# An attention and expert block on one core: the last rows kept on chip, first gathers split around the last tile, tables by large VectorE operations

## The chip, the core and the metric

One core of a Trainium2 chip runs the whole block as one program. Its engines have queues of their own: TensorE (PE, with the weight load shown apart as PEld), VectorE (DVE), ScalarE (ACT), GpSimd (POOL) and SyncE (SP), which only issues DMAs. The metric is the device time of one execution in microseconds, the median of several runs. All times below are microseconds unless they are marked ns.

## The reference, cut to what matters

The input is 32 samples of 256 tokens of 256 channels. A first part (a gate from a condition, causal attention over the 256 tokens of a sample, a low-rank conditioned layer) ends in rows `x` of 256 channels. The second part runs attention across the 32 samples at each token position, and then a layer of eight experts with a limit on the rows that each may take:

```python
attn = jax.nn.softmax(scores, axis=-1)
...
proj = jnp.einsum('sbh,oh->sbo', ao, proj_weight)
h1 = hidden_states + proj
ln2 = _layer_norm(h1, ln2_weight, ln2_bias)
...
probs = jax.nn.softmax(x @ router_weight, axis=-1)
top_p, top_i = jax.lax.top_k(probs, K)                 # K = 2 of E = 8
...
dst = jnp.where(within < cap, sorted_exp * cap + within, T)
...
fc1 = jax.nn.gelu(jnp.einsum('ech,ehf->ecf', xt, moe_w1))
fc2 = jnp.einsum('ecf,efh->ech', fc1, moe_w2).reshape(T, H)
...
return h1 + moe_out.reshape(S, B, H)
```

There are 8192 rows; each goes to its two best experts, 16384 rows of work, less those over the limit.

## The kernel before

**Stage 1** (loop at L476) handles one sample per step. It ends in a tile `o` of 128 partitions with the rows of the sample, two tokens to a partition, and POOL writes it to a DRAM array `xx_d[token, sample, :]` (L464). Three buffers `rows` hold `o` in turn.

**Stage 2** (loop at L1184, i from -13 to 64) works on 64 tiles of 128 rows, each 4 tokens x 32 samples. The order is written out by hand: at step i each helper is called for the tile for which it is due. Rows come back from `xx_d` in groups of four tiles, 16 groups in all; the first three (`EARLY`) have tiles of their own that exist already in stage 1, and their samples 0 to 27 are fetched ahead (`fetch_steps`, L107). When stage 2 begins, SP fetches samples 28 to 31 of these three groups, four DMAs a group at L111. A tile is then normalised on ACT (L762), turned and projected on PE, scored, masked on DVE (L820, L827) and POOL (L828), turned again (`turn_scores`, L837, and L842), multiplied with the values (L849) and put out (L883). Per group, `normalise2` and `judge` compute the second norm and the router's logits, and `rows2` and `store` write rows to DRAM for the experts.

**Placing the rows.** `route` picks the two best experts; it writes a 0/1 array `hot` for first and second choice. The place of each row within its expert's blocks is a running count. So that experts may start early, tiles 0 to 47 of the first ten samples (`SURE`) of each position are placed first: `packed(q)` compacts their choices onto 120 partitions with four small DMAs (L995), and `early()` counts them and makes the **first table**, the row numbers for the first eleven blocks of 256 rows (`EARLYB`). `rest()` does the same for all that is left, the **second table**. A table is made by matmuls: for eight row positions at a time, DVE makes a one-hot `oh` of the place within a block (L1125, L1438) and eight one-hots `wid` of the block multiplied with the row number, one operation each (L1132, L1446); a matmul for each position adds `oh` x `wid` into PSUM (L1140, L1431). The first table has 4 such groups, the second 16. Two integer operations (`rows_of`, L1164) then turn the sum into the row numbers `src_row` that a gather needs.

`early`, `rest`, `route` and `packed` are Python generators in a list `todo`. `advance(us)` emits their instructions into the stream until the costs that they yield come to its budget; a bare `yield None` ends that portion, so that the next matmul stands later than its input. At i = 61 whatever is left of the first table is emitted at once, and then the gathers of blocks 0 to 2 (POOL, L658, two indirect DMAs each) and the weights of block 0.

**Stage 3** (L1499, n from 0 to 19, `AHEAD`) computes one block of 256 rows a turn: `hidden(n)` (16 matmuls at L690 and two Gelus at L694), a gather for block n+3, `turn_in(n+1)` (L676 on PE, L680 on DVE), `weights(n+1)` (the expert's number is loaded into a register of DVE, and DVE copies 128 x 2048 floats at L668), `advance(HALF)`, `result(n)` (16 matmuls at L702, a copy on ACT at L706, a store by SP), and `advance(HALF)` again. At n = 10 (`EARLYB - 1`) the rest of the second table is emitted at once and the gathers of blocks 11 to 13 follow. Further blocks and the combining of each row's two results (`yg`, L1553) come behind.

Of the kernel before, what the change touches and what calls it, by code (L numbers as in the profile page):

```python
# [10 lines left out]
I32 = mybir.dt.int32  # L11
# [27 lines left out]
HALF = 2.4  # L39
# [10 lines left out]
def block_kernel(ctx: ExitStack, tc: tile.TileContext, a: dict, out: bass.AP):  # L50
# [56 lines left out]
    def fetch_steps(sg, lo, hi):  # L107

        src = xx_d[16 * sg : 16 * sg + 16].rearrange("(j b) s e -> b s j e", j=4)
        for b in range(4):  # L110
            nc.sync.dma_start(  # L111
                out=live2[sg]["xx"][32 * b + lo : 32 * b + hi], in_=src[b, lo:hi]
            )


    with ExitStack() as c1:
# [359 lines left out]
        for s in range(S + 1):  # L476
# [12 lines left out]
            if s == 5:  # L489
# [26 lines left out]
                with tc.tile_pool(name="cst", bufs=1) as cst:  # L516
# [14 lines left out]
                    for b in range(4):  # L531
# [12 lines left out]
                    icolf = cst.tile([P, P, 8], F32, name="icolf")  # L544
                    nc.gpsimd.iota(
                        icolf, pattern=[[1, P], [0, 8]], base=0, channel_multiplier=0,
# [12 lines left out]
                    icol = bf("icol_b", icolf)  # L559
                    irow = bf("irow_b", irowf)  # L560
                freshc = const.tile([P, NE, PACK], BF16, name="freshc")
# [4 lines left out]
                nc.vector.tensor_scalar(rowbits, rowbits, 16, None, ALU.logical_shift_left)  # L566

                rowbitsc = const.tile([P, PACK], I32, name="rowbitsc")
                for q in range(3):
                    for b in range(4):  # L570
                        r = SURE * (4 * q + b)
                        nc.sync.dma_start(
                            out=rowbitsc[r : r + SURE],
                            in_=rowbits[32 * b : 32 * b + SURE, PACK * q : PACK * (q + 1)],
                        )
# [41 lines left out]
            if s > 0:  # L617
                low_rank(s - 1)
            if s < S:
                transpose_p(s)  # L620
# [11 lines left out]
    hot = keep.tile([P, NJ, 2, NE], BF16, name="hot")  # L632
# [8 lines left out]
    hotc = keep.tile([P, PACK, 2, NE], BF16, name="hotc")  # L641
    slots1 = keep.tile([P, NJ, 2], F32, name="slots1")
    in1 = keep.tile([P, NE, 3 * PACK], BF16, name="in1")
    nc.gpsimd.memset(slots1, 0.0)
    nc.gpsimd.memset(in1, 0.0)

# [6 lines left out]
    ereg = nc.vector.alloc_register("ereg")  # L653
# [10 lines left out]
    def weights(n):  # L664
        eid, at_ = (eids[0], n) if n < EARLYB else (eids[1], n - EARLYB)
        nc.vector.load(ereg, eid[0:1, at_ : at_ + 1], bass_reorder=False)
        e = nc.vector.snap(ereg, min_val=0, max_val=NE - 1)
        nc.vector.tensor_copy(  # L668
            wcs[n % 2].rearrange("p a f -> p (a f)"),
            wall[:, bass.ds(e, 1), :, :].rearrange("p e a f -> p (e a f)"),  # L670
        )
# [58 lines left out]
    with ExitStack() as c2:  # L730
# [15 lines left out]
        def fetch(sg):  # L746
            if sg < EARLY:
                return fetch_steps(sg, 28, S)
# [186 lines left out]
        def route(first, n):  # L935
# [12 lines left out]
            revb = rev.unsqueeze(1).to_broadcast(je)  # L948
            left, val = lg, []
            cost = 0.22 if n > 8 else 0.19  # L950
            for k in range(2):
# [11 lines left out]
                nc.vector.tensor_tensor(hot[:, js, k, :], revb, over_e(rk), ALU.is_equal)  # L963
                yield cost
                if k == 0:
                    left = tmp("r_left", [NE])
                    nc.vector.scalar_tensor_tensor(
                        left, hot[:, js, 0, :], NEG, lg, ALU.mult, ALU.add
# [4 lines left out]
                both[:, :, js].rearrange("p e j -> p j e"), hot[:, js, 0, :], hot[:, js, 1, :],  # L973
                ALU.add,
# [14 lines left out]

        def packed(q):  # L990

            yield from route(PACK * q, PACK)
            for b in range(4):
                r = SURE * (4 * q + b)
                nc.sync.dma_start(  # L995
                    out=hotc[r : r + SURE],
                    in_=hot[32 * b : 32 * b + SURE, PACK * q : PACK * (q + 1)],
                )

        def early():  # L1000
# [11 lines left out]
            def by_expert(t):  # L1012
                return t[:, : NE * PACK].rearrange("p (e j) -> p e j", e=NE)

            ej = [NR, NE, PACK]

            def over_j(t):
                return t[:NR].unsqueeze(2).to_broadcast(ej)

            bothc, prec = cut(2 + NE * PACK, BF16), cut(NE * PACK, BF16)  # L1020
            nc.vector.memset(bothc[:, 0:1], 0.0)
            chosen = bothc[:, 1 : 1 + NE * PACK]
            nc.vector.tensor_tensor(
                by_expert(chosen)[:NR].rearrange("p e j -> p j e"), hotc[:NR, :, 0, :],
                hotc[:NR, :, 1, :], ALU.add,
            )
            yield 0.3
            nc.vector.tensor_tensor_scan(
                prec[:NR], bothc[:NR, : NE * PACK],
# [13 lines left out]
            for t in (prec, chosen):  # L1043
# [5 lines left out]
            yield None  # L1049
# [25 lines left out]
            ofk = yss[0].rearrange("p a b -> p (a b)")[:NR, : PACK * 2 * NE].rearrange(  # L1075
                "p (j k e) -> p j k e", k=2, e=NE
            )
            nc.vector.tensor_tensor(
                ofk, hotc[:NR],
                by_expert(slot)[:NR].rearrange("p e j -> p j e").unsqueeze(2)  # L1080
                .to_broadcast([NR, PACK, 2, NE]), ALU.mult,
            )
            yield 0.5
            n2 = 2 * PACK
            slots = cut(n2)
            nc.vector.tensor_reduce(
                slots[:NR].rearrange("p (j k) -> p j k", k=2), ofk, AX.X, ALU.add
            )
            none, col = cut(n2), cut(n2)
# [30 lines left out]
            for g in range(n2 // 8):  # L1120
# [10 lines left out]
                for i in range(8 * g, 8 * g + 8):  # L1131
                    nc.vector.tensor_scalar(  # L1132
                        wid[:NR, nbc * i : nbc * (i + 1)], irow[:NR, :nbc], col[:NR, i : i + 1],
                        rowbitsc[:NR, i // 2 : i // 2 + 1].bitcast(F32), ALU.is_equal, ALU.mult,
                    )
                    yield 0.1
# [11 lines left out]

        def split(pi, ci, hi, part, col, where):
# [9 lines left out]
            nc.vector.tensor_tensor(col, ci, hi, ALU.add)  # L1159
# [9 lines left out]
        def experts_of(late, cnt, cnti, diag, i=0, ps=None):  # L1169
# [10 lines left out]
            yield None  # L1180
# [3 lines left out]
        for i in range(-13, NJ + 1):  # L1184
# [8 lines left out]
            advance(0.2 if i < 3 * PACK + 2 else 1.2)  # L1193
            if 0 <= i + 3 < NJ:
                project(i + 3)
            if 0 <= i < NJ:
                values(i)
            if i == NJ:
# [11 lines left out]
            at(i, 5, normalise2)  # L1210
            at(i, 6, judge)
            for j in range(4):
                at(i, j + 6, rows2, j)
# [11 lines left out]
            if i == NJ - 3:  # L1225
# [9 lines left out]
                for n in range(3):  # L1235
                    gather(n)
                weights(0)
# [7 lines left out]
    with tc.tile_pool(name="rt", bufs=1) as rt, tc.tile_pool(  # L1245
# [8 lines left out]
        def by_tile(t):  # L1254

            return t.rearrange("p g e -> p e g").unsqueeze(3).to_broadcast([P, NE, NSG, 4])

# [9 lines left out]
        def rest():  # L1267
# [16 lines left out]
            yield None  # L1284
            kept = keptp[:, 1:].rearrange("p (e j) -> p e j", e=NE)
            nc.vector.scalar_tensor_tensor(
                keptp[:, 1:], p_row.rearrange("p e j -> p (e j)"), float(CAP), bothp[:, 1:],
                ALU.is_lt, ALU.mult,
            )
            yield 0.7  # L1290

            head = kept[:, :, : 3 * PACK]
            nc.vector.tensor_tensor(head, head, in1, ALU.subtract)
            yield 0.4
# [19 lines left out]
            yield None  # L1314
# [28 lines left out]
            last = [t1(f"last{i}", NSG + 1) for i in range(2)]  # L1343
            for t in last:
                nc.vector.memset(t[:, 0, :], 0.0)
            nc.vector.tensor_tensor(last[0][:, 1:, :], off, some, ALU.mult)
            yield 0.4
            step, at_ = 1, 0
            while step < NSG:
                src, dst = last[at_], last[1 - at_]  # L1350
                nc.vector.tensor_copy(dst[:, 1 : 1 + step, :], src[:, 1 : 1 + step, :])
                nc.vector.tensor_tensor(
                    dst[:, 1 + step :, :], src[:, 1 + step :, :],
                    src[:, 1 : NSG + 1 - step, :], ALU.max,
                )
                yield 0.4
                step, at_ = 2 * step, 1 - at_
            last = last[at_]
            jump = t1("jump")
            nc.vector.tensor_tensor(jump, last[:, 1:, :], last[:, :-1, :], ALU.subtract)  # L1360
# [4 lines left out]
            yield 0.5  # L1365
# [7 lines left out]
            nc.vector.tensor_tensor(slot4, slot4, by_tile(jump), ALU.mult)  # L1373
            yield 0.65
            nc.vector.tensor_tensor(slot4, slot4, by_tile(last[:, :-1, :]), ALU.add)
# [11 lines left out]
            jke = [P, NJ, 2, NE]  # L1387
            of_k = rt.tile(jke, F32, name="of_k")
            nc.vector.tensor_tensor(
                of_k, hot, slot.rearrange("p e j -> p j e").unsqueeze(2).to_broadcast(jke),  # L1390
                ALU.mult,
            )
            yield 1.9
            n2 = 2 * NJ
            slots = rt.tile([P, n2], F32, name="slots")
            nc.vector.tensor_reduce(
                slots.rearrange("p (j k) -> p j k", k=2), of_k, AX.X, ALU.add
            )
            yield 1.2
# [8 lines left out]
            col = rt.tile([P, n2], F32, name="col")  # L1408
            ints = [rt.tile([P, n2], I32, name=f"int{i}") for i in range(3)]
            split(*ints, part, col, where)  # L1410
            yield 1.2
# [14 lines left out]
            p_tab = rps.tile([P, nbc], F32, name="p_tab", tag="long")  # L1426
            ready = []
            for g in range(n2 // 8 + 1):
                for oh, wid, k in ready:
                    for i in range(8):  # L1430
                        nc.tensor.matmul(  # L1431
                            p_tab, lhsT=oh[:, :, i], rhs=wid[:, i, :],
                            start=(k == 0 and i == 0), stop=(k == n2 // 8 - 1 and i == 7),
                        )
                ready = []
                if g < n2 // 8:
# [3 lines left out]
                        part[:, 8 * g : 8 * g + 8].unsqueeze(1).to_broadcast([P, P, 8]),  # L1440
# [3 lines left out]
                    for i in range(8):  # L1444
                        j = 4 * g + i // 2
# [220 lines left out]
```

## Time and profile before

| | us |
|---|---|
| median of 3 runs | 1193.61 (1191.83 to 1194.23) |
| the profiled execution | 1260.33 |
| its span | 1258.6 |
| PE busy in it | 1118.8 (89%) |
| POOL busy | 539.4 (43%) |
| DVE busy | 702.3 (56%) |
| ACT busy | 399.5 (32%) |
| mean granted TensorE clock | 0.925 |

The profiled execution is one run, and it is 66.7 us longer than the median; what is read from it is compared with itself. Busy shares are averages over stages with different limits, so the stages are read one by one. These are the largest groups of instructions beside the ones for the tables; the columns are line, engine, operation, output and input with their shapes, count, then busy time and mean ns of one, then idle time of the engine just before and what ended most of it:

```profile
L702 PE MATMUL ps_y<-xx,ht 128*128 128x256 f32 x864 | 218.6, 410 | 48.1 <-ACT ht L694 41.1
L690 PE MATMUL ps_h<-xt,xx 128*128 128x256 f32 x864 | 197.9, 382 | 6.1 <-DVE xx L668 4.5
L658 POOL DMA_INDIRECT xx<-z_d,src_row x108 | 119.5, 1106 | 148.8 <-issue 83.1
L1553 POOL DMA_INDIRECT yg<-y_d,yrow x128 | 135.8, 1061 | 128.7 <-DMA y_d<-ys 67.8
```

A line names a tile by the buffer that it lies in: gathered rows and the expert weights use the memory of `xx`, and the first table's `oh` and `wid` that of `ht` and `xt`.

### The profile page before, as it was taken

To read this page: it belongs to the slowest core of one execution; us is meant where nothing else is said; L and a number is where in the kernel's file an instruction comes from. 1 tells how busy PE (TensorE), PEld (TensorE's weight loads), DVE (VectorE), ACT (ScalarE), POOL (GpSimd) and SP (SyncE) were. 2 spreads that over 40 slices of the span, in tenths; PEclk is the share of its full clock that TensorE was granted. 3 is DMA by queue.
4 is the path that set the end of the run, shared out by engine and by line. 5 is a ranking of instruction groups with operands and counts; after the bars stand their busy time and mean duration, and the time that the engine had idled before them with its cause. 6 is when DMAs were issued, how large, how long until landed. Compare 5 with 4: busy or idle time off the path is not lost. (4 is left out here: it accounts for less than half of the span.)

```text
span 1258.6 us, 17522 instructions
## 1 busy us (share of the span) xinstructions
PE 1118.8 (89%) x5926; PEld 913.4 (73%) x5926; DVE 702.3 (56%) x1781; ACT 399.5 (32%) x958; POOL 539.4 (43%) x798
## 2 busy tenths in 40 slices
PE   5999999999994999999988699989987996688692
PEld 4988888888872777777766488768876875566581
DVE  5135555555552888888899868842223543233342
ACT  2023333333333566666654122112211221111120
POOL 4012222222222566666665452043254775754562
PEclk8589999999997999999999699979997997988896
DMA  9023333333253143443341141022233663553554
GB/s 327 10 64 103 120 113 109 102 108 120 73 144 115 36 149 123 170 166 116 129 159 46 60 138 55 27 69 73 76 106 113 204 189 103 155 152 114 152 167 128
DMA packets 84867, 147.45 MB, mean 117 GB/s; under 512 B 11272, under 2 KB 51360, under 8 KB 84256
## 3 DMA queue, kind: packets, MB, share of 16 engines
q1 hardware_dynamic: 68832, 97.92, 23.9%
q0 software_dynamic: 15936, 48.32, 12.7%
q8 instruction: 49, 0.80, 0.3%
q14 instruction: 50, 0.41, 0.1%
HBM read 89.39 MB, written 56.69 MB: 116 GB/s over the span
## 5 line engine op out<-in xcount | busy, mean ns | idle before, releaser
L702 PE MATMUL ps_y<-xx,ht 128*128 128x256 f32 x864 | 218.6, 410 | 48.1 <-ACT ht L694 41.1
L702 PEld LDWEIGHTS ps_y<-xx,ht 128*128 128x128 f32 x864 | 174.0, 207 | 78.8 <-ACT ht L694 45.7
L680 DVE TENSOR_SCALAR xt<-ps_xt,ln 128x256 f32<-128x256 f32 x106 | 52.8, 541 | 273.7 <-PE ps_xt L676 139.9
L690 PE MATMUL ps_h<-xt,xx 128*128 128x256 f32 x864 | 197.9, 382 | 6.1 <-DVE xx L668 4.5
L1553 POOL DMA_INDIRECT yg<-y_d,yrow x128 | 135.8, 1061 | 128.7 <-DMA y_d<-ys 67.8
L690 PEld LDWEIGHTS ps_h<-xt,xx 128*128 128x128 f32 x864 | 164.6, 191 | 31.1 <-DVE xx L668 5.6
L658 POOL DMA_INDIRECT xx<-z_d,src_row x108 | 119.5, 1106 | 148.8 <-issue 83.1
L706 ACT COPY ys<-ps_y 128x512 f32<-128x512 f32 x54 | 31.7, 587 | 272.9 <-PE ps_y L702 125.7
L694 ACT ACTIVATE ht<-ps_h 128x512 f32<-128x512 f32 x108 | 63.8, 598 | 145.4 <-PE ps_h L690 85.8
L94 POOL TENSOR_SCALAR ve<-mv 128x2 f32<-128x2 f32 (+2 forms) x49 | 10.8, 220 | 221.0 <-DVE mv L102 219.8
L778 PE MATMUL p_qkv<-wqkv,lnt 128*128 128x384 f32 x256 | 94.5, 493 | 0.0
L828 POOL TENSOR_TENSOR sc<-sc,mx 128x512 f32<-128x512 f32 x64 | 67.7, 1058 | 53.1 <-DVE mx L827 46.0
L849 PEld LDWEIGHTS p_av<-vbd,pt 128*128 128x128 f32 x512 | 68.0, 196 | 27.4 <-ACT pt L842 13.1
L788 ACT COPY vbd<-p_qkv 32x64 f32<-32x64 f32 x256 | 52.9, 207 | 91.1 <-DVE qk L784 88.8
L849 PE MATMUL p_av<-vbd,pt 128*128 128x68 f32 x512 | 67.0, 275 | 8.1 <-ACT pt L842 5.9
L883 PE MATMUL p_pr<-wp,ao 128*128 128x264 f32 x256 | 72.7, 407 | 0.0
L340 PE MATMUL p_z<-yt,m_qk 128*128 128x256 f32 x256 | 69.3, 396 | 1.3 <-ACT yt L329 1.3
L668 DVE COPY xx<-wall 128x2048 f32 x54 | 66.8, 1236 | 1.4 <-DMA xx<-z_d,src_row 1.4
L888 POOL TENSOR_TENSOR res<-h,xx 128x256 f32<-128x256 f32 x64 | 43.8, 685 | 51.8 <-DVE h L887 51.6
L453 PE MATMUL p<-layer,x1t 128*128 128x264 f32 x256 | 64.0, 393 | 0.8 <-ACT x1t L443 0.7
L369 DVE TENSOR_TENSOR layer<-p_l,base 128x264 f32<-128x264 f32 x64 | 24.7, 428 | 69.7 <-PE p_l L364 69.7
L349 PE MATMUL p_v<-w_vo,yt 128*128 128x256 f32 x256 | 61.2, 382 | 0.0
(301 smaller groups left out, 1981.3 us busy)
## 6 DMA issues: line engine op xcount, KB each, us to landing
xx_d<-o POOLq DMA_DIRECT2D x32, 530.0 KB
y_d<-ys SPq DMA_DIRECT2D x54, 256.0 KB
xx<-xx_d SPq DMA_DIRECT2D x13, 1060.0 KB
xt<-in_x_t_dram SPq DMA_DIRECT2D x32, 256.0 KB
xs<-in_x_dram SPq DMA_DIRECT2D x32, 256.0 KB
wall<-in_moe_w_dram SPq DMA_DIRECT2D x16, 512.0 KB
z_d<-h SPq DMA_DIRECT2D x16, 512.0 KB
res_d<-res SPq DMA_DIRECT2D x16, 512.0 KB
```

The source lines that it names most:

```text
L340: nc.tensor.matmul(p_z[:, m, :], lhsT=m_qk[:, c, m * P : (m + 1) * P], rhs=yt[:, c, :], start=(c == 0), stop=(c == 1),)
L453: nc.tensor.matmul(p_2, lhsT=v["x1t"][:, c, t * P : (t + 1) * P], rhs=v["layer"][:, c, :], start=(c == 0), stop=(c == 1),)
L658: nc.gpsimd.indirect_dma_start(out=xgs[n % 4][:, h, :], out_offset=None, in_=z2_d[: 3 * PACK * P, :] if n < EARLYB else z2_d[:, :], in_off ...
L668: nc.vector.tensor_copy(wcs[n % 2].rearrange("p a f -> p (a f)"), wall[:, bass.ds(e, 1), :, :].rearrange("p e a f -> p (e a f)"),)
L690: nc.tensor.matmul(ps[:, i, :], lhsT=we1[:, c, f * P : (f + 1) * P], rhs=xts[n % 2][:, c, :], start=(c == 0), stop=(c == 1),)
L694: nc.scalar.activation(hts[n % 2][:, 2 * f2 : 2 * f2 + 2, :], ps, AF.Gelu_apprx_tanh)
L702: nc.tensor.matmul(ps[:, h, :], lhsT=hts[n % 2][:, f, h * P : (h + 1) * P], rhs=we2[:, f, :], start=(f == 0), stop=(f == 3),)
L778: nc.tensor.matmul(ps, lhsT=live2[n // 4]["lnt"][:, c, j * P : (j + 1) * P], rhs=wqkv[:, c, :], start=(c == 0), stop=(c == 1),)
L828: nc.gpsimd.tensor_tensor(sc, sc, mx.unsqueeze(2).to_broadcast([P, 16, S]), ALU.subtract)
L849: nc.tensor.matmul(p_a[:, g // 2, :, g % 2, :], lhsT=v["pt"][:, g, :], rhs=vbd[n % 5][:, g], start=True, stop=True,)
L883: nc.tensor.matmul(p_p, lhsT=tiles[n]["ao"][:, gp, :], rhs=wp2[:, gp, :], start=(gp == 0), stop=(gp == 1),)
L1553: nc.gpsimd.indirect_dma_start(out=yg, out_offset=None, in_=y_d[:upto, :], in_offset=bass.IndirectOffsetOnAxis(ap=yrow[:, j, k : k + 1], a ...
```

## The change

**The last rows.** At the end of stage 1, samples 28 to 30 of the first three groups are fetched from DRAM, those of the first group on the ACT queue and the others on SP. Sample 31 isn't read back: twelve small DMAs copy it from its tile on chip to the three groups. `fetch` in stage 2 leaves these groups out.

**The tables.** `hot` becomes `hot1`, which holds only the first choice; the second is had by subtraction. `packed` moves two arrays instead of one (eight DMAs). The eight `wid` operations of a group become two, `columns` (a comparison) and `numbered` (a multiplication with the row numbers, now in bf16); in the first table all four groups share one pair of them. In the second table the groups are made in pairs with the matmuls of a pair one portion later. A chain of four copies and maxima becomes one scan, and some bare yields are gone.

**The order.** `advance` comes behind `project` and `values`, with 1.4 instead of 1.2, and `HALF` is 3.2 instead of 2.4. At i = 61 only block 0 is gathered. The gathers of blocks 1 and 2, the weights of block 0 and a new subtraction on POOL (`other`) stand at i = 63, and two helpers of the last groups are moved by a step or two.

**The weights.** For the first eleven blocks the register is loaded and the weights are copied by ACT, for the later ones by DVE as before.

```diff
-HALF = 2.4
+HALF = 3.2
...
+            if s == S:
+                for sg in range(EARLY):
+                    fetch_steps(sg, 28, S - 1, nc.sync if sg else nc.scalar)
+
+                for sg in range(EARLY):
+                    for b in range(4):
+                        (nc.sync if sg or b % 2 else nc.scalar).dma_start(
+                            out=live2[sg]["xx"][32 * b + S - 1 : 32 * (b + 1)],
+                            in_=rows[(S - 1) % 3][16 * sg + b : 16 * (sg + 1) : 4, 0, :],
+                        )
...
-        nc.vector.load(ereg, eid[0:1, at_ : at_ + 1], bass_reorder=False)
-        e = nc.vector.snap(ereg, min_val=0, max_val=NE - 1)
-        nc.vector.tensor_copy(
+        i = int(n >= EARLYB)
+        eng, copy = ((nc.scalar, nc.scalar.copy), (nc.vector, nc.vector.tensor_copy))[i]
+        eng.load(eregs[i], eid[0:1, at_ : at_ + 1], bass_reorder=False)
+        e = eng.snap(eregs[i], min_val=0, max_val=NE - 1)
+        copy(
...
-                nc.sync.dma_start(
-                    out=hotc[r : r + SURE],
-                    in_=hot[32 * b : 32 * b + SURE, PACK * q : PACK * (q + 1)],
-                )
+                for t, u in ((both, by_expert(bothc[:, 2:])), (hot1, hot1c)):
+                    nc.sync.dma_start(
+                        out=u[r : r + SURE],
+                        in_=t[32 * b : 32 * b + SURE, :, PACK * q : PACK * (q + 1)],
+                    )
...
+        def columns(out, col, n):
+
+            k = col.shape[1] // 2
+            dims = [col.shape[0], k, n // 2, 2]
+            nc.vector.tensor_tensor(
+                out.rearrange("p (k n h) -> p k n h", k=k, h=2),
+                irow[: dims[0], :n].rearrange("p (n h) -> p n h", h=2).unsqueeze(1)
+                .to_broadcast(dims),
+                col.rearrange("p (k h) -> p k h", h=2).unsqueeze(2).to_broadcast(dims),
+                ALU.is_equal,
+            )
+
+        def numbered(rows, bits):
+
+            k = bits.shape[1]
+            rows = rows.rearrange("p (k n h) -> p k n h", k=k, h=2)
+            nc.vector.tensor_tensor(
+                rows, rows, bits.unsqueeze(2).to_broadcast(rows.shape), ALU.mult
+            )
...
-            advance(0.2 if i < 3 * PACK + 2 else 1.2)
             if 0 <= i + 3 < NJ:
                 project(i + 3)
             if 0 <= i < NJ:
                 values(i)
+            advance(0.2 if i < 3 * PACK + 2 else 1.4)
...
-                for n in range(3):
+                gather(0)
+            if i == NJ - 1:
+                weights(0)
+                for n in range(1, 3):
                     gather(n)
-                weights(0)
+                nc.gpsimd.tensor_tensor(other, both[:, :, : 3 * PACK], in1, ALU.subtract)
...
-            for g in range(n2 // 8 + 1):
-                for oh, wid, k in ready:
...
+            for g in range(0, n2 // 8 + 2, 2):
+                for r in ready:
+                    passes(*r)
                 ready = []
-                if g < n2 // 8:
+                for k in range(g, min(g + 2, n2 // 8)):
...
-                    for i in range(8):
-                        j = 4 * g + i // 2
-                        nc.vector.tensor_scalar(
-                            wid[:, i, :], irow[:, :nbc], col[:, 8 * g + i : 8 * g + i + 1],
-                            rowbits[:, j : j + 1].bitcast(F32), ALU.is_equal, ALU.mult,
-                        )
-                    yield 1.5
-                    ready.append((oh, wid, g))
-                    if g % 2 or g == n2 // 8 - 1:
-                        yield None
+                    rows = wid.rearrange("p i n -> p (i n)")
+                    columns(rows, col[:, 16 * k : 16 * k + 16], nbc)
+                    numbered(rows, rb2[:, 4 * k : 4 * k + 4])
+                    ready.append((oh, wid, k))
+                    yield 1.8
+                yield None
```

## The prediction, made before the changed kernel was run

> **What bounds the kernel now.** I read the engine totals first: TensorE is busy for 1118.8 of 1258.6 us, so the time is its work plus its pauses, and only a pause can be won. The row of slices shows where they are. Each digit is the share in tenths of 31.5 us, so a digit under 9 is a pause:
>
> ```profile
> PE   5999999999994999999988699989987996688692
> ```
>
> The 4 at slice 12 is the change of stage. The dips at slices 20 to 22 are the end of stage 2 and the first table of rows, the 8 at 25 is the second table, and the late ones lie among the experts, which the change hardly touches. The view of windows prices them. Its columns are window, length, busy time of PE, of the weight load, of VectorE, ScalarE and GpSimd, then granted TensorE clock and DMA:
>
> ```profile
> 384.00:395.00 11.00, 0.00 (x0) 0.00 (x0) 0.00 (x0) 0.02 (x1) 2.08 (x7) 0.50 0.26 72
> 420.00:640.00 220.00, 220.00 (x1460) 168.57 (x1458) 191.59 (x464) 136.74 (x359) 142.62 (x242) 1.00 0.41 142
> 636.80:690.80 54.00, 46.95 (x304) 34.05 (x302) 49.97 (x132) 24.85 (x70) 29.28 (x51) 1.00 0.23 77
> 690.80:728.30 37.50, 24.73 (x118) 19.30 (x117) 27.96 (x97) 6.99 (x13) 17.01 (x25) 0.68 0.16 50
> 728.30:802.50 74.20, 72.87 (x388) 63.27 (x387) 58.05 (x161) 17.62 (x31) 22.41 (x22) 1.00 0.26 89
> 802.50:830.80 28.30, 20.29 (x113) 15.40 (x112) 24.00 (x90) 2.53 (x5) 3.79 (x4) 0.76 0.08 24
> ```
>
> The 220 us of full tiles have no pause: a tile takes 4.52 us and VectorE has some 0.7 us of it to spare. From 636.8 to 728.3 VectorE is the limit (49.97 of 54.0), and at 802.5 again. So the change works in three places, at 384, 637 to 728 and 802. I price each against the profiled execution (1260.33 us, 1.7 more than its span). That run lies 67 us above the median of 1193.61, mostly in long pauses after 920 us; the three places lie ahead of them, so I carry the gain over whole.
>
> **Part 1, the change of stage.** The timeline (start, duration, instruction, idle time before it and its releaser):
>
> ```profile
> 385.16 0.81 POOL L464 DMA_DIRECT2D xx_d<-o  x1 [0.30 <-POOL o L463]
> 388.55 6.50 SPq L111 DMA_DIRECT2D xx<-xx_d  x12
> 394.98 1.59 ACT L762 ACTIVATE z<-xx 128x256 f32<-128x256 f32 x3 [15.22 <-DMA xx<-xx_d]
> ```
>
> Stage 2 waits for the last sample's rows to go to DRAM (385.16 to 388.55) and return through twelve fetches, 0.54 us to issue each; the first group's fourth is issued at 390.2, and its data is used at 394.98, 4.8 us on. After the change rows 28 to 30 need only sample 30's write, landed near 381.7. Sample 31's rows go straight from the tile on the chip, complete at 384.86. ScalarE, idle until 394.98, issues four of the first group's and two of its last copies (385 to 386); SP issues the other eight fetches (381.7 to 386), then two copies to 387.1. Landing takes 3.1 us (write end to the first semaphore) to 4.5 us, so the data is there near 391: **4 us** gained. Here a rule speaks against the change: the Trainium skill, "DMA: Bandwidth & Descriptors", section "Issuing engines are not separate DMA queues", says that issuing from several engines shares the same DMA engines and saves only issue time, usually small beside the transfer. By the rule the second queue is worth about nothing, and the removed DRAM trip (3.4 us) alone pays. The row has 6.5 us of issue against some 4 of landing, so it isn't small; I take 4 instead of 3. The bounds are 0 (a stage 2 buffer waits for memory that the late copies still read; 24 are issued until about 391) and 6.
>
> **Part 2, the end of stage 2.** In the chain here, `L837` turns the scores of a tile, `L1132` is the first table and `L668` the weights:
>
> ```profile
> 698.92 1.66 DVE L1132 TENSOR_SCALAR xt<-irow_b,z,rowbitsc 120x22 bf16<-120x22 bf16 x8
> 705.07 1.08 PE L837 MATMUL ps_t<-ident,sc 128*128 128x128 f32 x4
> 710.17 1.23 DVE L668 COPY xx<-wall 128x2048 f32 x1 [1.35 <-DMA xx<-z_d,src_row]
> 715.16 1.11 PE L837 MATMUL ps_t<-ident,sc 128*128 128x128 f32 x4 [4.42 <-POOL sc L828]
> ```
>
> Before: tile 61 starts at 690.8, tile 62 14.3 us later because the table is drained at i=61, tile 63 10.1 after that (its mask sits behind the weight copy on VectorE and six gathers on GpSimd), and the first result 13.1 later, at 728.3. After: counting the generator's steps with its new costs, the table is complete at i=60, so the drain finds nothing. I take 5.2, 4.4 and 13.4 us, the last 0.3 longer because two gathers and the 0.8 us subtraction now stand ahead of the residual on GpSimd. That wins 14.5.
>
> But the work comes into tiles 51 to 60. They took 54.0 where PE alone needs 45.2; the 8.8 over it plus ten slacks of 0.7 is 15.8 us of added VectorE time. Now come four comparisons (4 x 0.68 = 2.7), the two large operations for 704 elements (about 0.52 each, 1.05) and some of the router's next pass (1.6); the dropped `chosen` and the longer slot sums cancel. Add 1.5 for waiting on the 32 table matmuls, 0.7 for a two-input operation held while GpSimd works (1.10 us for a 128-element one at L1070), and a **new wait**: the scan at i=53 needs eight compacting DMAs, not four. The four of L995 take 3.02 us to issue, so eight take 6, and the last lands some 8 us after the tile's start, but VectorE is at the scan after 3.8, so about 3.7 is lost; queued behind the scan are the next mask and the query copies. Sum 27.0, less 7 of slack: 20.0 over 45.2, against 8.8. It gives back 11.2, so **3.3 us** stay. The bounds are +9 (no scan wait, slack used better) and -4 (both the DMA wait and contention doubled).
>
> **Part 3, the second table.**
>
> ```profile
> L1438 DVE TENSOR_TENSOR oh<-icol_b,part 128x1024 bf16<-128x1024 bf16 x16 | 11.1, 692 | 0.0
> L1446 DVE TENSOR_SCALAR wid<-irow_b,col,rowbits 128x126 bf16<-128x126 bf16 x128 | 30.2, 321 | 0.0
> 826.04 0.95 POOL L658 DMA_INDIRECT xx<-z_d,src_row  x1 [57.14 <-issue]
> 830.81 5.42 PE L702 MATMUL ps_y<-xx,ht 128*128 128x256 f32 x16
> ```
>
> A group is one `oh` and eight `wid`, spaced at 2.39 us. Six of sixteen are drained at n=10 while PE runs dry, and the next result starts 28.3 us after the transpose at 802.5. The rule against it: "VectorE: DVE Perf Modes" of the Trainium skill, section "The perf-mode tier table (the rule you actually need)", has a two-tensor operation stop at two elements a cycle where a one-tensor operation reaches four. By the rule, and since there are now two passes over 1008 elements, the swap costs more. But 321 ns for 126 elements is mostly fixed cost, and eight take 1.9. The nearest row for the new operations is `oh`, of the same kind and size, 0.692: by length 0.68 each, so the group is 2.05 busy, about 1.9 spaced. At one element a cycle it would be 1.2 each, group 3.0. I take 0.68: the pairs keep the innermost run contiguous as in `oh`. The first groups then come at n=3 instead of 5, fourteen are done by n=9, two remain. From the transpose of n=10: passes to 5.6, hidden to 9.1, passes to 12.0, row numbers 12.9, gather 13.5, result 4.8 later at 18.3; **10.0 us** less. Three more groups' passes come before 802.5 (1.44 for two, so 2.2), a wait on the expert count of 0.5 and less cold clock go the other way: 8.6 net. The bounds are 4 and 11. What is late next is the gather, 4.8 us that nothing shortens.
>
> **The weights on ScalarE.** `ys` takes 587 ns for 512 elements and `vbd` 207 for 64: 0.85 an element, so 1.9 us for 2048 against 1.24 on VectorE. They stand behind both Gelus of a block and are done about 2.9 us after them; the hidden layer needs them 4.2 after. Result copies queue behind, with over 3 us to spare. ScalarE is busy for 17.6 of 74.2. Cost nothing; without that cover 0.65 x 11 = 7.
>
> **The rest**, smaller index tables and setup under full stage 1 work, fewer small operations: nothing. Sum 4 + 3.3 + 8.6 = 15.9: 1260.3 to about 1244.4, and the median to **1178**.
>
> **Rivals.**
> *More* (0.17): the scan does not wait and the boundary gives 6: 6 + 7 + 9.5 = 22.5, 1171. For: VectorE's order before the scan isn't tight. Against: eight small DMAs in one queue.
> *Mostly given back* (0.17): late buffers at the boundary (1), early table -1, one element a cycle (5): 1188.5. For: tiles 51 to 60 already run on VectorE.
> *Slower* (0.05): the weight copy on ScalarE becomes the limit of a block. It decides beyond about 4.3 us from the second Gelu; at 6 us eleven blocks lose 1.7 each, 19, so 15.9 turns into -3: 1197. Against: it would need three times the rate of its rows.
> *Not doing what it says* (0.06): the pauses after 920, 10 to 20 us each and not explained by a release, fall differently and cover the gain: 1188 to 1200.
>
> My forecast has 0.55, its own range 1172 to 1184. The range of 1167 to 1191 reaches over both near rivals. A measurement of this kernel can tell about 0.2% from no change; the cases give 0.87 faster, 0.05 within, 0.08 slower.
>
> **What would show it.** First `z` near 391; the scan at i=53 idle for some 3 to 4 us on a compacting DMA; no matmul of the first table between tiles 61 and 62, and tile 62 about 5 us after 61; second table groups spaced at 1.9 with 0.68 a large operation, two of them left at n=10, result 18 after the transpose; the ScalarE weight copy near 1.9 and no wait of the hidden layer on it. The prediction is wrong if the tiles 51 to 60 take over 75 us, or the large operations over 1 us.

## The result and the profile after

The changed kernel takes 1177.15 us (median of 4 runs, 1176.11 to 1181.11) against 1193.92 before: ratio 0.9866, 95% interval 0.9837 to 0.9894, 16.8 us less. The forecast was 1178. The profiled execution has a span of 1174.4 us. The total was right, in part by luck: by the positions below, part 1 gave 3.4 us less than forecast and parts 2 and 3 gave 2.7 and 4.3 more, while the time moved 2.7 less than the parts add up to.

The row of slices of the changed kernel (a slice is 29.4 us) and its windows, with the same columns as before: tiles 51 to 60; tiles 61 and 62; tile 63 to the first result; blocks 0 to 8; block 9 to 10:

```profile
PE   5999999999999599999999788998999999999891
```

```profile
637.06:697.07 60.01, 48.65 (x336) 36.60 (x334) 52.87 (x145) 25.26 (x70) 29.59 (x51) 1.00 0.21 69
697.07:707.48 10.41, 6.06 (x42) 4.50 (x40) 9.37 (x28) 1.68 (x3) 5.63 (x7) 1.00 0.37 133
707.48:722.52 15.04, 11.57 (x44) 9.14 (x45) 6.32 (x24) 6.71 (x10) 10.55 (x18) 0.77 0.12 37
722.52:796.50 73.98, 72.92 (x415) 63.91 (x414) 50.34 (x110) 34.23 (x41) 17.59 (x23) 1.00 0.27 90
796.50:812.70 16.20, 11.10 (x87) 9.86 (x86) 11.23 (x29) 4.14 (x6) 3.78 (x4) 0.97 0.13 42
```

The tiles at 637 are slower than before (54.0), still on VectorE; tiles 61 and 62, which had 24.4 us with a clock near 0.65, now take 10.4 at full clock; block 9 to 10 fell from 27.9 to 16.2. Set beside the two profiles, in us:

| step | forecast | measured |
|---|---|---|
| last write of stage 1 to the first tile's turned scores | 4 less | 21.94 to 21.38: 0.6 less |
| tiles 51 to 60 | 11.2 more | 53.99 to 60.01: 6.0 more |
| tile 61 to 63 | 14.8 less | 24.37 to 10.41: 14.0 less |
| tile 63 to the first result | 0.3 more | 13.14 to 15.04: 1.9 more |
| first result to that of block 9 | 1.4 more | 74.62 to 73.98: 0.6 less |
| block 9 to 10 | 10.0 less | 27.89 to 16.20: 11.7 less |
| block 10 to 11 | 0 | 9.14 to 8.56: 0.6 less |
| sum | 15.9 less | 19.5 less |

Three things the numbers need. Stage 1 itself ended 0.8 later in this execution, so block 11 starts 18.7 earlier. Two rows of the table also move between executions of the kernel before: in its second profile (`b_again`, below) tiles 51 to 60 take 56.75 and tile 63 to the first result 15.34, so that the gain from the last write to block 11 is 17 to 25 us, by the pair of profiles that is taken. And executions differ by some 80 us from one occasion to another, the kernel before included (1276 and 1272 us in the first two sets of runs below, 1194 in the third), nearly all of it behind block 11. So ratios are given against the kernel before of the same set, and the readings rest on positions ahead of block 11.

### The profile page after: what moved, and what is told of

The parts are those of the page before. It is cut to its first block, busy times and chain, and to the rows that moved or that the text cites. A ratio compares the mean times of both kernels' runs of the same rounds, so it can differ in the third digit from the quotient of the medians.

```text
span 1174.4 us, 17424 instructions
## 1 busy us (share of the span) xinstructions
PE 1083.7 (92%) x5926; PEld 894.6 (76%) x5926; DVE 674.0 (57%) x1641; ACT 419.8 (36%) x969; POOL 539.1 (46%) x800
## 4 chain that ended last, share of the span: by engine, by line
PE 73%; issue 9%; DMA 7%; DVE 6%; POOL 3%; SPq 1%; ACT 1%; POOLq 0%; DVEq 0%; ACTq 0%
PE ps_h L713 10%; PE ps_y L725 9%; PE p_qkv L801 6%; PE p_z L340 5%; PE p L453 5%; PE p_v L349 5%; PE p_pr L906 4%; PE p_av L872 4%; DMA yg<-y_d,yrow 4%; PE p_sc L831 3%; PE ps_t L860 3%; PE p_o L422 3%; DMA xx<-z_d,src_row 3%; PE p_s L389 2%; POOL yg L1608 2%
## 5 line engine op out<-in xcount | busy, mean ns | idle before, releaser
L725 PE MATMUL ps_y<-xx,ht 128*128 128x256 f32 x864 | 200.2, 386 | 0.0
L679 POOL DMA_INDIRECT xx<-z_d,src_row x108 | 124.1, 1149 | 134.5 <-issue 66.5
L725 PEld LDWEIGHTS ps_y<-xx,ht 128*128 128x128 f32 x864 | 163.6, 194 | 21.1 <-ACT ht L717 0.3
L801 PEld LDWEIGHTS p_qkv<-wqkv,lnt 128*128 128x128 f32 x256 | 44.7, 195 | 18.6 <-issue 1.2
```

The lines of the kernel that those rows point to most:

```text
L679: nc.gpsimd.indirect_dma_start(out=xgs[n % 4][:, h, :], out_offset=None, in_=z2_d[: 3 * PACK * P, :] if n < EARLYB else z2_d[:, :], in_off ...
L725: nc.tensor.matmul(ps[:, h, :], lhsT=hts[n % 2][:, f, h * P : (h + 1) * P], rhs=we2[:, f, :], start=(f == 0), stop=(f == 3),)
L801: nc.tensor.matmul(ps, lhsT=live2[n // 4]["lnt"][:, c, j * P : (j + 1) * P], rhs=wqkv[:, c, :], start=(c == 0), stop=(c == 1),)
```

## The experiments

### Which part of the time is the kernel's

`b_again` is the kernel before once more; `after_again` and `after_third` are the changed kernel, each for the runs beside it.

> The kernel before, unchanged, for a second profile: that of the prediction was 67 us above its median. Theory (the 67 us are pauses of that one execution after 920 us, and the change wins only ahead of block 11): span near 1192, the start of block 11's result near 840 as in the first profile, and from there to the end some 352 us, as the changed kernel has (821.3 to 1174.4, 353). Rival (the change also shortens the tail, by its later loads of the weights or less traffic): from block 11 to the end 360 us or more.

It took 1283 us. Its block 11 starts at 849.3, 9 us later than in the first profile (stage 1's last write is 4 late, tiles 53 and 54 are 3 longer, and tile 63 to the first result 2 longer), and 432 us lie behind it, against 419 in the first profile. My theory of one bad execution fell. So did the rival, though its sign came: the changed kernel has 432 there too (`after_again`), so the long tail goes with the occasion.

> The changed kernel once more, on one chip with the next three, so that they can be set beside it. Theory (its gain lies ahead of block 11, whatever the chip): ratio to the kernel before 0.984 to 0.988; last write of stage 1 to first z 8.8 us, tile 53's period 8.3, first result to that of block 9 74.0, block 9 to 10 16.2. Rival (the step from block 3 to 4, 8.7 in the first profile and 11.7 in two of the experiments, differs from run to run of one kernel): that step is 11.7 here too.

> The changed kernel, for the run above. Theory: ratio to the kernel before 0.984 to 0.988, and the positions of its stages within 1.5 us of its two earlier profiles.

The ratios were 0.9848 (0.9784 to 0.9913) and 0.9846 (0.9822 to 0.9870). The positions held within the bounds, but for block 1 to 2 of `after_again`, 9.25 in place of 8.05, where VectorE waited 2.9 for a signal of PE. From block 11 to the end it was 432 and 355. Where the 432 go can be seen in a pause, here from the timeline of `e2_group_by_group` (described below), at a result copy of ScalarE:

```profile
1021.22 0.59 ACT L727 COPY ys<-ps_y 128x512 f32<-128x512 f32 x1 [15.09 <-remote]
```

The copy waits for two marks, that of the store that last read its buffer, two blocks back, and TensorE's. TensorE's came at 1021.15, 12 us after the recorded end of the matmuls that it stands for (1009.0). The last landing that the trace has of that store is at 995.56, and its record is incomplete. What made the signal late isn't shown.

### The change of stage

The timeline of the changed kernel, and what SP's queue waited for (total, times, longest):

```profile
382.57 8.64 SPq L111 DMA_DIRECT2D xx<-xx_d  x8
382.60 1.51 ACTq L111 DMA_DIRECT2D xx<-xx_d  x4
385.94 0.81 POOL L464 DMA_DIRECT2D xx_d<-o  x1 [0.30 <-POOL o L463]
386.37 2.40 ACTq L633 DMA_DIRECT2D xx<-o  x2
391.32 6.22 SPq L633 DMA_DIRECT2D xx<-o  x10
394.77 2.07 ACT L785 ACTIVATE z<-xx 128x256 f32<-128x256 f32 x4 [14.24 <-DMA xx<-o]
```

```profile
SPq L111 <- DMA xx<-xx_d: 5.5, 1, 5.5
```

ACT issues four DMAs in 1.5 us, SP eight in 8.6, and the first group's last two copies wait behind these until 391.32. The trace names the mark on which each DMA completes. There are eight (101 to 108), which SP and ACT share, and one is taken again only when its last DMA has landed (mark 105 at 388.95):

```
start   queue  line  waits for mark
382.57  SP     L111  (write of sample 30)
382.85  SP     L111  102
383.17  SP     L111  104
383.48  ACT    L111  105
388.97  SP     L111  105   <- held until ACT's DMA of 383.48 had landed
```

Two runs tell this from slow transfers. The first undoes part 1 (diffs are cut where `...` stands):

```diff
-            if sg < EARLY:
-                return
+            if sg < EARLY:
+                return fetch_steps(sg, 28, S)
...
-            if s == S:
-                ...
```

> The changed kernel with part 1 undone: samples 28 to 31 of the first three groups come from DRAM in twelve SP fetches after sample 31's write. Theory (part 1 wins nothing, since its DMAs hold one another up on shared completion marks): the first tile of stage 2 starts within 1 us of the changed kernel's (394.8), the time is 1177 within 1.5 us. By the prediction's step, part 1 was worth 4 us: 1181. Rival (part 1 costs): under 1175.

Ratio 0.9838 (0.9798 to 0.9877). From the last write to the first `z` it takes 9.7 us (8.8 in the changed kernel), to the first turned scores 21.9 (21.4): part 1 as written is worth 0.3 to 0.6 us (the changed kernel's three profiles have 21.4 to 21.6). The second keeps the 24 DMAs and changes their order:

```diff
                 for sg in range(EARLY):
                     fetch_steps(sg, 28, S - 1, nc.sync if sg else nc.scalar)
-
-                for sg in range(EARLY):
                     for b in range(4):
```

> The changed kernel with the same 24 DMAs, but each group's four copies of sample 31 right behind its fetches, so that SP issues the first group's two copies before the other groups' fetches. Theory (SP stood still for 5.5 us at its fourth fetch because the completion mark it was to use was still that of an ACT fetch in flight, and the first group's last copies were queued behind): the copies go out near 386.4 on SP and, where ACT waits for its own marks, by 388.5; first z near 391.5 in place of 394.8; time 1174. Rival (the copies or fetches are simply slow to land beside the write of sample 31): first z stays near 394.5, time 1177.

```profile
386.69 1.29 SPq L631 DMA_DIRECT2D xx<-o  x2
386.69 1.53 ACTq L631 DMA_DIRECT2D xx<-o  x2
391.45 2.08 ACT L783 ACTIVATE z<-xx 128x256 f32<-128x256 f32 x4 [9.90 <-DMA xx<-o]
```

Lines here are two lower than in the changed kernel. SP's copies leave at 386.69, and `z` starts 4.5 us after the last write, not 8.8; the turned scores come 18.9 after it, 2.4 sooner than in the changed kernel and 3.0 sooner than with part 1 undone. The rival falls: the copies were as quick as I had taken them (the last of the first group landed 3.7 us after its issue), the queue was held. At block 11 nothing is left of it: block 3 to 4 took 11.74 instead of 8.69 (see the last experiments). In the time (ratio 0.9857, 0.9812 to 0.9901) it could not be seen.

### The scan's wait

```diff
-            for b in range(4):
-                r = SURE * (4 * q + b)
-                for t, u in ((both, by_expert(bothc[:, 2:])), (hot1, hot1c)):
+            for t, u in ((both, by_expert(bothc[:, 2:])), (hot1, hot1c)):
+                for b in range(4):
+                    r = SURE * (4 * q + b)
```

> The changed kernel with the four DMAs of the counts (bothc) ahead of the four of the first choices (hot1c) in each compaction. Only the counts are an input of the scan. Theory (VectorE's 3.39 us of idle time before the scan at tile 53 is on the path): idle time under 0.5, tile 53's period 8.3 to about 5.2, time 3 us less, 1174. Rival (slack in the next tiles takes it up, or PE binds there): the scan starts as early, but tile 61 starts less than 1 us earlier and the time stays at 1177.

The scan in the changed kernel, then in this one:

```profile
657.27 0.43 DVE L1049 TENSOR_TENSOR_SCAN z<-bothc,freshc 120x128 bf16<-120x128 bf16 x1 [3.39 <-DMA hot1c<-hot]
```

```profile
656.06 0.43 DVE L1049 TENSOR_TENSOR_SCAN z<-bothc,freshc 120x128 bf16<-120x128 bf16 x1 [0.79 <-DMA hot1c<-hot]
```

With the counts first (the releaser's name is inferred), the idle time falls by 2.6, tile 53's period goes from 8.29 to 5.69, and tiles 51 to 60 from 60.0 to 57.4. All of it arrives at tile 61: the wait was on the path there. Here too block 3 to 4 took 11.75, so block 11 comes no sooner. Ratio 0.9870 (0.9822 to 0.9918), again too wide for it.

### What the second table's gain is made of

```diff
-                    columns(rows, col[:, 16 * k : 16 * k + 16], nbc)
-                    numbered(rows, rb2[:, 4 * k : 4 * k + 4])
+                    for i in range(8):
+                        j = 4 * k + i // 2
+                        nc.vector.tensor_scalar(
+                            rows[:, nbc * i : nbc * (i + 1)], irow[:, :nbc],
+                            colf[:, 8 * k + i : 8 * k + i + 1],
+                            rowbits[:, j : j + 1].bitcast(F32), ALU.is_equal, ALU.mult,
+                        )
```

> The changed kernel with the second table's two large operations taken back to eight small ones a group (one more small operation makes their float operand); budgets, pairs and order stay. Theory (the prediction's sizes, 2.39 against 1.92 a group, but exposed only where VectorE has no slack, which is the two groups left at block 10, and each table matmul waiting for its own operation): blocks 4 to 9 at 8.8 in place of 8.4, +2.4 in all, block 9 to 10 1 to 1.5 longer, sum +3.5 to +4. Rival (the swap itself makes most of part 3's gain): +8 or more. Other rival (its size doesn't matter, the order does): under +1.

The groups of instructions, first of the changed kernel, then of this one:

```profile
L1187 DVE TENSOR_TENSOR wid<-wid,rb 128x1008 bf16<-128x1008 bf16 x16 | 10.9, 683 | 0.6
L1175 DVE TENSOR_TENSOR wid<-irow_b,col 128x1008 bf16<-128x1008 bf16 x16 | 10.8, 676 | 0.0
```

```profile
L1510 DVE TENSOR_SCALAR wid<-irow_b,colf,rowbits 128x126 bf16<-128x126 bf16 x128 | 30.0, 312 | 0.0
```

VectorE is busy 8.3 us more (30.0 against 21.7), and block 9 to 10 is 0.96 longer than in `after_again` (17.11 against 16.15), blocks 0 to 9 0.15. So the swap is worth 1.1 here; beside the other two profiles of the changed kernel it would be 2.3, the difference lying in block 1 to 2, which varies between runs. My +2.4 for the blocks missed: they stay at 8.38, since the matmuls of a pair stand a portion behind its operations and no longer wait for each. Ratio 0.9895 (0.9830 to 0.9960).

The next run gives the weights back to VectorE:

```diff
-        i = int(n >= EARLYB)
+        i = 1
```

> The changed kernel with the weights of the first eleven blocks copied by VectorE as before. Theory (VectorE is the limit only in blocks 1 to 3, where the counts for the second table are made and PE waited 1.1 us for them at block 4): block 3 to 4 2 to 3.5 us longer, the other blocks and block 10 as in the changed kernel; +2 to +3.5. By the prediction (the move costs and wins nothing): 0. Rival (VectorE falls behind in each block with a table group, 1.24 each): +7 or more.

```profile
716.70 1.23 DVE L691 COPY xx<-wall 128x2048 f32 x1 [0.64 <-DVE xt L703]
717.99 3.78 PE L713 MATMUL ps_h<-xt,xx 128*128 128x256 f32 x8 [4.25 <-DVE xx L691]
```

```profile
757.29 0.23 PE L1225 MATMUL p_eid<-diag,ones_b 128*128 128x128 bf16 x1 [3.49 <-DVE diag L1220]
```

PE now waits for the copy at block 0 (first result 18.4 us after tile 63; 15.6 in `after_again`) and at block 4, where it waits 3.49 for the counts. In the changed kernel that matmul is

```profile
750.59 0.23 PE L1225 MATMUL p_eid<-diag,ones_b 128*128 128x128 bf16 x1 [1.06 <-DVE diag L1220]
```

Block 3 to 4 takes 12.81 instead of 8.69, and block 9 to 10 0.6 more. That step is not the slow one of other runs (see the last experiments), in which VectorE stands 2.4 to 3.0 us for PE: here it stands 0.5, and then runs with one gap of 0.17 from 743 to 757, with two of the copies (1.23 each) in it. Block 11 comes 7.0 us later after the last write (444.7 against 437.7). The last rival's size, but not its place: it comes at block 0 and in the blocks in which VectorE makes the counts, and the blocks with groups have room. About 1 us of block 0 is a lower granted clock there, 0.67 against 0.76. In the time (ratio 0.9893, 0.9814 to 0.9972) little of it shows: behind block 11 this run had 418 us and `after_again` 432.

The last of these runs takes back the larger share of table work in a block:

```diff
-HALF = 3.2
+HALF = 2.4
```

> The changed kernel with the share of a block that table work gets back at 2.4 (it is 3.2 in the change). Counting the generator's steps, the first pair of groups moves from block 3 to block 4, and four groups instead of two are left at block 10. Theory (each group left costs 1.9 there, and PE's 1.1 us wait for the counts at block 4 goes away): block 9 to 10 some 3.8 longer, 20.0; blocks 0 to 9 2 us shorter in all (one pair of matmul groups less, 1.0, and the wait); net +2. Rival (the larger share is what part 3 lives on): +6 or more.

Block 9 to 10 is 18.44 instead of 16.12 (`after_third`), blocks 0 to 9 72.67 instead of 73.98: some 0.6 of my estimate on both sides, net 1.0. That two more groups cost 2.3 and not 3.8 there fits table matmuls that run beside the groups. 1179.07 us, ratio 0.9879 (0.9849 to 0.9909), against 1176.21 for `after_third`. The rival of +6 falls.

### The split of the first gathers

```diff
-                gather(0)
+                for n in range(3):
+                    gather(n)
             if i == NJ - 1:
                 weights(0)
-                for n in range(1, 3):
-                    gather(n)
```

> The changed kernel with the gathers of blocks 0, 1 and 2 all issued after step 61 again; weights and the subtraction stay at step 63. Theory (six gathers of 1.25 us each stand on GpSimd ahead of the mask of tile 63): tile 62 to 63 5.8 to about 10, but the first result 1 to 2 us sooner after tile 63, since GpSimd is free then; net +2.5 to +3.5 at the first result. Rival (the split wins nothing: what it saves before tile 63 it pays behind): within 1 us.

```profile
711.16 0.95 POOL L679 DMA_INDIRECT xx<-z_d,src_row  x1 [0.30 <-issue]
712.13 1.06 POOL L851 TENSOR_TENSOR sc<-sc,mx 128x512 f32<-128x512 f32 x1
713.25 1.12 PE L860 MATMUL ps_t<-ident,sc 128*128 128x128 f32 x4 [7.36 <-POOL sc L851]
```

The mask follows the sixth gather at once, PE waits 7.36 for it, and tile 63 comes 10.81 after tile 62 (5.80 in `after_third`). The first result follows 14.2 after it, 1.1 sooner; net 3.9, a little over my range. My reason for the 1.1 does not hold: up to the first hidden matmul it takes 0.6 longer, although GpSimd is free, and the 24 matmuls behind it take 1.7 less, at a granted clock of 1.00 instead of 0.77. The kernel takes 1181.52 us, ratio 0.9902 (0.9871 to 0.9933), against 1176.21.

### Both orders together

> The changed kernel with both reorderings: each group's copies right behind its fetches, and the counts ahead of the first choices in each compaction. Theory (the two waits are independent and both on the path): first tile turned 2.5 to 3 us earlier, tile 53's period 5.7, first result some 5.6 us earlier than in the changed kernel on the same chip; 3 of it may be lost again at block 4 if its table counts come later than PE. Time 2.5 to 5.5 us under the changed kernel's. Rival (both are taken up by later waits): within 1 us of it.

> Both reorderings once more, beside the changed kernel on the same chip. Theory: by the trace block 11's result starts 5 to 6 us earlier after the last write of stage 1; where the experts' part has no pauses the time is 4 to 6 us under the changed kernel's, where it has them (pauses of 10 to 20 us that end on a DMA) the difference can't be seen in the times.

`e7_both_orders` carries the diffs of `e2_group_by_group` and `e3_counts_first`. In the first run the tile's period was 5.70, and the first result came 9.9 sooner after the last write than in `after_again`. That is more than the two waits: 4.8 lie ahead of the turned scores, about 2.0 of them because six projections took 2.20 and not 4.21 us as in `e2_group_by_group`; 2.6 are the scan's; and 2.5 come behind tile 63, at a granted clock of 0.87. 1.8 of it was lost again in blocks 0 to 9 (block 3 to 4 took 11.39), and block 11 came 7.3 sooner. Its ratio, 0.9840 (0.9786 to 0.9895), is that of `after_again`: behind block 11 lay 436 us and 432. In the third set it took 1171.97 us (1168.65 to 1173.70) against 1176.21 (1173.98 to 1179.83) for `after_third`: all six runs lie under all six of the changed kernel. The first result comes 5.8 sooner after the last write, within my 5 to 6 for block 11. Block 11 itself comes 7.4 sooner, but the other 1.6 lie in block 10 to 11, which varies by 1.4 in the changed kernel's own profiles. Ratio to the kernel before 0.9811 (0.9787 to 0.9835). It beats both kernels, by 22 and by 4 us.

Block 3 to 4 took 11.4 to 11.8 us in three runs of these orders (`e2_group_by_group`, `e3_counts_first`, `e7_both_orders`) and 8.69 in `e7_again`, the same program as the third. In the slow ones VectorE (2.4, 2.4 and 3.0 us; 1.4 in `e7_again`) and ScalarE (4.4, 4.3 and 2.9; 2.2) both stood for a signal of PE, after which the counts were late. What held the signal isn't shown, so the rival in `after_again`'s expectation, that the step differs between runs of one kernel, is borne out for this kernel and open in its cause.

## Why the prediction was right, and where it wasn't

- **What bounds it.** Right: pauses at three places, all ahead of block 11, and VectorE in two of them.
- **Part 1, 4 us: wrong.** The term that failed is the issue of the DMAs at 0.54 us each, "SP issues the other eight fetches (381.7 to 386), then two copies to 387.1". They came at 391.3, held by a completion mark of the other queue. Landing was near the estimate of 3.1 to 4.5 for the first group's copies (2.4 to 4.6), but ACT's fetch on that mark took 5.5. The profile of before had a sign of it: its last four of twelve fetches stood near 1 us apart, the first eight 0.34, and the ninth left at 391.66, when the first one's mark came free. I divided 6.50 by 12 and lost that, and so had the first group's fourth fetch at 390.2, where the trace has 389.53. The rule on issuing engines and the row both missed the marks: in the order as written the second queue gains nothing, since it takes marks that SP needs. In the order of `e2_group_by_group` part 1 is worth 3.0 at the turned scores; what of it is the second queue's wasn't tried.
- **Part 2, 3.3 us: right in most of its mechanisms, 2.7 off in sum** (6.0 against the first profile; 10.5 to 11.0 against `b_again`, whose tiles 51 to 60 and first result are slower). The scan's wait was as forecast (3.7 in the sum; 3.39 idle, 2.6 worth by `e3_counts_first`). The waits on 32 table matmuls (1.5) didn't come: in these tiles VectorE waits for PE 0.8 us in all, none of it at an operation of the table. And "contention, 0.7 more" had the wrong sign: five small operations that took 0.9 to 1.1 in the tiles before, while GpSimd masked, were mostly near 0.2 to 0.5 after; two of the four comparisons still took 0.97 and 1.10 instead of 0.68, beside GpSimd operations. That fits `advance` behind the projection and not right behind the mask, but wasn't tried alone. The slack of 0.7 a tile is 0.58 by the row of full tiles; it drops out of the sum. Tiles 61 to 63 and the empty drain came as said (tile 61 to 62 from 14.28 to 4.62); `e8_gathers_together` gives the split of the gathers 5.0 at tile 63 and 3.9 at the first result.
- **Tile 63 to the first result, 0.3 longer: not settled.** It took 1.9 more than in the first profile, and I had left the clock out. The windows from the first hidden matmul to the first result, in that profile, in the changed kernel's and in `b_again`:

```profile
722.49:728.30 5.81, 5.12 (x24) 4.12 (x25) 2.41 (x10) 1.74 (x4) 2.11 (x4) 1.00 0.00 0
```

```profile
715.07:722.52 7.45, 6.76 (x24) 5.33 (x25) 2.13 (x9) 1.74 (x4) 6.34 (x8) 0.77 0.23 70
```

```profile
729.82:737.83 8.01, 7.32 (x24) 5.78 (x25) 2.42 (x10) 1.74 (x4) 2.11 (x4) 0.72 0.00 0
```

  The same 24 matmuls take 5.12, 6.76 and 7.32 at a granted clock of 1.00, 0.77 and 0.72. So the kernel before has both: the whole step takes 13.14 in its first profile and 15.34 in its second, against 15.04 to 15.56 in the changed kernel's three. The clock decides here, but that the change lowers it is not shown; what sets it in one execution isn't either.
- **Part 3, 8.6 us: 12.9.** The large operations are 0.68, as read from the nearest row. From the transpose of n=10 to its result it was 16.6, not 18.3: the last 32 matmuls ran together in 2.1 us. Four groups, not three, moved ahead of the result of block 9, and two of them in a block cost 1.03 in place of 1.44. By the timelines this is where the gain comes from: eight groups, 2.39 apart, stand behind that result in the kernel before, and four, 1.92 apart, in the changed one, 9.6 and 1.9 us against the measured 11.7. The larger `HALF` accounts for two of the four groups (`e6_smaller_share`) and for 1.0 net; the other two, which the new costs and pairs moved, weren't tried alone. The swap itself is worth 1.1 to 2.3 of the 12.9 (`e4_eight_small`), though the rule that spoke against it was rightly set aside: two large operations keep VectorE busy for less time than eight small ones. The sum of 8.6 also had a gap: 10.0 less 2.2 and 0.5 is 7.3, and the 1.3 for a less cold clock was not worked out.
- **The weights on ScalarE, "cost nothing": right on ScalarE** (1.89 us, estimate 1.9), **wrong on VectorE**: I asked what the move costs and not what it frees. It is worth about 7 (`e5_weights_on_dve`, one profile), at block 0 and at the counts of block 4. That my "without that cover" came to 7 as well is chance: it had 0.65 in each of eleven blocks.
- **Carrying the gain over whole** held: 16.8 in the first set, 17.8 in the third. That block 11 moved by 18.7 and the time by 1 to 2 less isn't explained; two profiles of the kernel before differ by 5 us on the way to block 11. Undone one at a time, the parts give 0.5 (part 1), 3.9 (gathers), 1.1 (swap), 7 (weights) and 1 (`HALF`), 13.5 in all; the emptied drain is read from the traces alone.
- **The rivals.** The slower one fell with the copy's 1.89 us, and "mostly given back" with the 0.68 of the large operations, though its boundary of 1 us was nearer than my 4. Of "more", the step of the scan without a wait did not come by the change; `e7_again` is that case made.

## What to carry to other kernels

Count DMAs that are in flight, not only their issue time: where two queues share a few completion marks, a DMA of one can stop the other, and whatever the next stage needs first must be issued ahead of that. Price a moved operation at both ends, on the engine that takes it and on the one that loses it, and look for the stretch in which the second is the limit. And where executions vary more than an edit is worth, compare positions in the trace up to the stage that varies.

## What was not expected of the hardware

The eight marks above, with 5.5 us of waiting. And the experts' part: from block 11 to the end 350 to 355 us in five profiles of the changed kernel and its variants and 418 to 436 in seven others on other occasions, with pauses of 10 to 20 us. Some end on a DMA, others on a signal of TensorE that comes long after the recorded end of its matmuls (12 us in the one above). There the end hardly follows the start: block 11 at 817.0 gave a span of 1253.4 (`e7_both_orders`), at 831.2 one of 1249.3 (`e5_weights_on_dve`). What makes an occasion slow isn't shown; it is not the chip as such, since the record names chip 11 both for the set at 1276 and for the one at 1194.
